# Value projection of two head pairs: from eight half products to seven, over the sums that queries and keys use

## The chip, the cores and the metric

The kernel runs on one NeuronCore of a Trainium2 chip. The metric is the device time of one execution in microseconds (us). Engines are named as the profile names them: PE is TensorE (matmul), PEld its weight loads, DVE is VectorE, ACT is ScalarE, POOL is GpSimd, SP is SyncE, which here only issues DMA transfers.

## What is computed

Two layers, each over four images of 1024 positions and 768 channels, all in float32:

```python
x = x + attention(_gn(x), ...)     # layer 0, then layer 1 with its own weights
# attention: q, k, v = split(xn @ Wqkv), 12 heads of 64
# scores = scale * q @ k.T + rel_h[..., :, None] + rel_w[..., None, :]
# out = softmax(scores) @ v ;  return out @ Wproj + bproj
```

`_gn` is a group normalisation over 32 groups of channels. The change concerns `v`, the values, alone.

## The kernel before, in words

**Units.** Heads go in pairs: `g` counts 48 pairs (8 images by 6 pairs, `NP`), and `pair` is the number within the image. A pair is worked in eight units `n` of 128 query rows. While unit (g, n) runs, the kernel also makes queries, keys and values of the next pair g + 1 and a part of the output projection. All engines run in the order in which the code emits their instructions (`tc.manual_schedule`); the Tile framework adds the semaphore waits.

**A unit, in the order of emission** (L740 to L826): DVE "between" instructions for groups that stand half done; the transfers collected in `early`; POOL's bias sums for two units ahead (`biases`, L429); the score matmuls of the next unit (L443) and their softmax (`exponentials`: DVE L455, ACT L459); then the first "piece" of projection work; `turn` (two DVE transposes L479 and the transfer of the result to DRAM, L481); `divide` for the next unit (DVE reciprocal L467, then products on ACT L473, one of the two on POOL L471 where n is 2 or 4 for the unit divided); POOL's weight differences (`combine` at n 0 and 1, `combine_values` at n 4 of odd pairs); the other pieces; and at n 2 and 6 `weigh`, the product of probabilities and values (L508, result `av`). At n 2 the position terms of the next pair (`positions`: 16 matmuls `tp`, L381, and the ACT copies `t` L386 and `raw` L389) stand ahead of the scores, at n 7 behind them.

**Pieces.** `plan` (L733) says which groups run in which unit: G0 to G3 are the four products of queries and keys (tile `pj`), V0 and V1 the values (tile `pv`), O0 and O1 the output projection (`oo`). A group made by `crossed` has two parts. In its first part, rows 0 to 63 of the array feed one half of the result tile and rows 64 to 127 the other; in the second part they change over. Ahead of the second part, `between` (L274) has DVE rewrite one element of a weight with itself, which makes PE wait until the first part has been read.

**Values before.** For every two head pairs, `project_values` makes four groups (i = 0 to 3), two of them beside an even pair and two beside an odd one. A group covers 256 positions by 256 output columns; each of its two parts has 12 matmuls of 64 rows x 256 moving columns, weights being the input `xn`. Two ACT copies (L366) bring the result into `v_of[g]` and `v_of[g + 1]`.

**Queries and keys** use a seven-product scheme: POOL makes differences of weights (`combine`, L129) and of inputs (`sums`, L257: s2, s3, s4 and an in-place x1 + x1), and DVE adds the products (L329). The sums of the next image are made at pairs 4 and 5 (`sum_steps`); s4 comes last, its three tiles at n 1 and n 2 of pair 5; before, its first reader is G3 at n 4.

**Places in PSUM.** The score tiles have two places (`ps_s`). Everything else (`pj`, `pv`, `oo`, `tp`, `av`) shares two places of pool `ps_m`. In the built program, a new tile takes the place that has been free longest. At n 2, group V1 stands half done and holds one of the two, so `tp` and then `av` take the other in turn.

**Transfers.** Each unit writes its transposed probabilities to DRAM (`td<-tb`, 1 MB) and reads them back one to three units later in another order (`pt<-td`, 1 MB, L490), all from SP in order; `weigh` at n 6 needs the reads of units 0 to 3.

## Time and profile before

| what | value |
|---|---|
| median of 3 runs | 3369.71 us (3365.89 to 3370.19) |
| profiled execution, own time | 3373.25 us |
| its span, first to last instruction | 3370.8 us |
| around the span | 2.45 us |
| PE / DVE / ACT / POOL busy | 98% / 72% / 61% / 69% |
| values: PE `pv`, 4608 records | 523.5 us |
| values: ACT copies L366, 192 | 59.8 us |
| values: POOL L140, 24 | 43.9 us |
| one pair of heads | 68.72 us in nearly all pairs |

The profile's first part gives the busy time of each engine; groups give line, engine, tiles, count, busy time and mean time of one; the timeline lists merged runs of instructions in order, with the start in us from the span's start, the duration, and in brackets the idle time of the engine before them and what ended it. One float32 matmul appears as two PE records. Matmuls on the upper and the lower 64 rows of the array run at once, so two records start almost together.

### The profile page before, as it was taken

To read this page: it belongs to the slowest core of one execution; us is meant where nothing else is said; L and a number is where in the kernel's file an instruction comes from. 1 tells how busy PE (TensorE), PEld (TensorE's weight loads), DVE (VectorE), ACT (ScalarE), POOL (GpSimd) and SP (SyncE) were. 2 spreads that over 40 slices of the span, in tenths; PEclk is the share of its full clock that TensorE was granted. 3 is DMA by queue.
4 is the path that set the end of the run, shared out by engine and by line. 5 is a ranking of instruction groups with operands and counts; after the bars stand their busy time and mean duration, and the time that the engine had idled before them with its cause. 6 is when DMAs were issued, how large, how long until landed. Compare 5 with 4: busy or idle time off the path is not lost.

```text
span 3370.8 us, 58086 instructions
## 1 busy us (share of the span) xinstructions
PE 3319.2 (98%) x21600; PEld 1875.8 (56%) x21600; DVE 2415.5 (72%) x3923; ACT 2039.6 (61%) x3140; POOL 2332.4 (69%) x1184
## 2 busy tenths in 40 slices
PE   6999999999999999999999999999999999999998
PEld 3555555555555555555555555555555555555554
DVE  3787677777777677777777777667776677767775
ACT  2666756566565666566655666566665657665563
POOL 5777866678666686666866668676686667766662
PEclk9999999999999999999999999999999999999999
DMA  3899989899998998889888999989998999898887
GB/s 113 297 330 312 336 306 338 319 306 335 321 322 314 315 331 312 312 300 334 320 309 315 316 321 330 317 306 313 337 313 308 334 306 335 301 324 299 312 290 263
DMA packets 534777, 1046.97 MB, mean 311 GB/s; under 512 B 149728, under 2 KB 212704, under 8 KB 485344
## 3 DMA queue, kind: packets, MB, share of 16 engines
q1 hardware_dynamic: 479936, 1015.84, 85.6%
q10 hardware_dynamic: 54560, 27.43, 2.8%
q8 instruction: 171, 2.80, 0.3%
q14 instruction: 110, 0.90, 0.1%
HBM read 568.01 MB, written 475.10 MB: 309 GB/s over the span
## 4 chain that ended last, share of the span: by engine, by line
PE 93%; DMA 4%; DVE 2%; issue 1%; ACT 0%; SPq 0%; POOL 0%; ACTq 0%; DVEq 0%
PE pj L285 21%; PE av L508 19%; PE s L443 19%; PE pv L285 15%; PE oo L285 13%; PE pj L313 3%; PE tp L381 3%; DMA td<-tb 2%; DMA pt<-td 1%; PE o L587 1%; DVE tb L479 1%; DMA xn<-in_x 0%; DVE sc L455 0%; DVE st L188 0%; DMA per<-mv 0%
## 5 line engine op out<-in xcount | busy, mean ns | idle before, releaser
L429 POOL TENSOR_TENSOR sc<-rel 128x1024 f32<-128x1024 f32 x768 | 1880.3, 2478 | 636.8 <-DVE tb L479 601.6
L455 DVE CUSTOM_DVE_ANT_0 sc<-s,sc 128x1024 f32<-128x1024 f32 x768 | 910.9, 1225 | 524.0 <-PE s L443 459.5
L459 ACT ACTIVATE sc<-sc,sm 128x1024 f32<-128x1024 f32 x768 | 878.5, 1146 | 484.9 <-DVE sm L455 483.8
L473 ACT ACTIVATE sc<-sc,sm 128x1024 f32<-128x1024 f32 x674 | 743.0, 1143 | 580.3 <-DVE sm L467 454.1
L479 DVE STREAM_TRANSPOSE tb<-sc 128x1024 f32<-128x1024 f32 x768 | 909.6, 1226 | 60.9 <-DMA td<-tb 56.8
L443 PE MATMUL s<-k,q 64*128 64x512 f32 x3072 | 738.6, 596 | 2.6 <-DVE sm L455 2.6
L508 PE MATMUL av<-pt,v 128*64 128x256 f32 x6144 | 687.5, 381 | 10.1 <-DMA pt<-td 9.0
L508 PEld LDWEIGHTS av<-pt,v 128*64 128x64 f32 x6144 | 436.2, 137 | 290.6 <-issue 48.5
L285 PE MATMUL pv<-wv,xn 64*128 64x256 f32 x4608 | 523.5, 376 | 1.0 <-DVE wv L274 1.0
L285 PEld LDWEIGHTS pv<-wv,xn 64*128 64x128 f32 x4608 | 447.7, 187 | 114.5 <-issue 55.2
L285 PE MATMUL oo<-attn,wo 64*128 64x512 f32 x2112 | 475.3, 589 | 0.0
L443 PEld LDWEIGHTS s<-k,q 64*128 64x128 f32 x3072 | 289.2, 187 | 316.1 <-issue 292.5
L285 PEld LDWEIGHTS oo<-attn,wo 64*128 64x128 f32 x2112 | 200.9, 187 | 228.0 <-issue 227.1
L471 POOL TENSOR_SCALAR sc<-sc,sm 128x1024 f32<-128x1024 f32 x94 | 105.1, 1118 | 305.7 <-DVE sm L467 295.6
L285 PE MATMUL pj<-xn,wa 64*128 64x512 f32 x1152 | 269.4, 598 | 30.6 <-DVE xn L235 26.7
L285 PE MATMUL pj<-xn,w 64*128 64x512 f32 x1152 | 263.3, 589 | 1.6 <-DVE w L274 1.6
L285 PE MATMUL pj<-s,wc 64*128 64x512 f32 x576 | 262.6, 589 | 0.0
L285 PE MATMUL pj<-s,w 64*128 64x512 f32 x576 | 262.6, 589 | 0.0
L285 PEld LDWEIGHTS pj<-xn,wa 64*128 64x128 f32 x1152 | 113.6, 189 | 166.5 <-issue 126.7
L285 PEld LDWEIGHTS pj<-xn,w 64*128 64x128 f32 x1152 | 111.6, 187 | 137.4 <-issue 134.9
L404 ACT COPY rel<-raw 32x256 f32<-32x256 f32 x384 | 155.1, 404 | 30.6 <-DMA part<-res 10.9
L285 PEld LDWEIGHTS pj<-s,wc 64*128 64x128 f32 x576 | 107.6, 187 | 67.6 <-issue 66.9
(68 smaller groups left out, 2118.5 us busy)
## 6 DMA issues: line engine op xcount, KB each, us to landing
td<-tb SPq DMA_DIRECT2D x384, 1024.0 KB, 6.6
pt<-td SPq DMA_DIRECT2D x382, 1024.0 KB, 9.0
tdr<-t ACTq DMA_DIRECT2D x96, 256.0 KB, 6.5
part<-res SPq DMA_DIRECT2D x84, 256.0 KB, 5.0
res<-part SPq DMA_DIRECT2D x84, 256.0 KB, 4.7
wa<-in_wqk SPq DMA_DIRECT2D x48, 384.0 KB, 3.3
wc<-in_wqk SPq DMA_DIRECT2D x48, 384.0 KB, 6.3
wv<-in_wv SPq DMA_DIRECT2D x24, 768.0 KB, 12.4
```

Source lines behind the costliest of these rows:

```text
L285: nc.tensor.matmul(to, lhsT=w, rhs=x, start=(half, at) == (0, 0), stop=(half, at) == (1, n - 1))
L313: nc.tensor.matmul(t[:, h, :], lhsT=w[rows, c, :], rhs=x[c][rows, :], start=(c == 0), stop=(c == NB - 1),)
L381: nc.tensor.matmul(ps[:, h, j, :], lhsT=q[rows, at * P : (at + 1) * P], rhs=tabs[l][rows, :], start=True, stop=True,)
L404: nc.scalar.copy(rel[rows, :, 0, :, :], raw[rows, :, :, WIDE - 1 - HW - y : WIDE - 1 - y])
L429: nc.gpsimd.tensor_tensor(sc.rearrange("p (a k) (u l) -> p a (k u) l", a=4, l=8), rel[:, h, 0, m, :].unsqueeze(1).unsqueeze(3).to_broadcas ...
L443: nc.tensor.matmul(ps[h][:, cols], lhsT=q[rows, n * P : (n + 1) * P], rhs=k[rows, cols], start=True, stop=True,)
L455: nc.vector.tensor_tensor_reduce(out=sc, in0=ps[h], in1=sc, scale=-scale, scalar=BIG, op0=ALU.add, op1=ALU.min, accum_out=st[:, 0, h : h + 1],
L459: nc.scalar.activation(sc, sc, AF.Exp, bias=st[:, 0, h : h + 1], scale=-1.0, accum_out=st[:, 1, h : h + 1],)
L471: nc.gpsimd.tensor_scalar(sc, sc, st[:, 2, h : h + 1], 1.0, ALU.mult, ALU.mult)
L473: nc.scalar.mul(sc, sc, st[:, 2, h : h + 1])
L479: nc.vector.transpose(tb[:, :, h, :], sc_of[g, n, h])
L508: nc.tensor.matmul(av[rows, at * 2 * P : (at + 1) * 2 * P], lhsT=v_of[g][:, k, rows], rhs=pt_of[g, quarter].rearrange("p n r k h i -> p (n ...
```

## The change

The values of two pairs (512 positions a half, 128 columns a pair, 384 channels a half) are made by the same seven-product scheme as queries and keys, with the same sums s2, s3, s4 and x1. `values` has kinds 0 to 3. Kinds 0, 1 and 2 are crossed groups with two products each, kind 3 is a single product without crossing. A product covers 512 positions by 128 columns over 384 channels, in matmuls of 64 rows x 128 moving columns; a crossed part has 24 of them, kind 3 has 24 in all. Beside an odd pair run kinds 0 (V0) and 3 (V1), beside an even pair kinds 1 (V0) and 2 (V1) of the two pairs begun before. The results are put together in the v tiles: kind 0 by one ACT copy and one DVE add, kind 3 by two DVE adds, kinds 1 and 2 by three DVE adds each (128 x 512).

The weight differences, one POOL subtraction of 128 x 768 before, become four of 128 x 384, two at n 3 and two at n 5 of an odd pair, with a new tile `wv2`. The order of pieces now depends on the pair: beside an odd pair, V1 no longer begins at n 1 and runs whole at n 3, behind G1. To make room, the small tile `g` of the normalisation moves into the place of `raw`. `between` touches an element of the moving operand for values (`kept` = 2), as it did. At the start of the program the order of the groups changes likewise.

```diff
-        wv_of[g] = w
+        wv_of[g] = w, wpool.tile([P, NB, P], FP, tag="wv2", name=f"wv2_{g}")
...
-    def combine_values(g):
-
-        w = wv_of[g]
-        nc.gpsimd.tensor_tensor(w[:, NB:], w[:, NB:], w[:, :NB], ALU.subtract)
+    def combine_values(g, stage):
+
+        w, t2 = wv_of[g]
+        sub = lambda to, x, y: nc.gpsimd.tensor_tensor(to, x, y, ALU.subtract)
+        w11, w21 = w[:, :NB, :P], w[:, NB:, :P]
+        w12, w22 = w[:, :NB, P:], w[:, NB:, P:]
+        if stage == 0:
+            sub(w11, w12, w11)
+            sub(w12, w22, w12)
+        else:
+            sub(t2, w22, w11)
+            sub(w21, w21, t2)
...
-        g = small.tile([NG, 2, GS, 2], FP, tag="g", bufs=1, name=f"g_{im}")
+        held = []
...
+            window = tmppool.tile([P, 2, 4, WIDE], FP, tag="raw", name=f"g_{im}")
+            g = window.rearrange("p h j r -> p (h j r)")[:NG, : 4 * GS]
...
-    def project_values(g, i):
+    def values(g, kind):
...
-        t = ps_m.tile([P, 2, HALF], FP, tag="m", name=f"pv_{g}_{i}")
-        yield from crossed(t, range(NC), lambda t, c, k, rows: (
-            t[:, k, : 2 * P], xn[c][rows, (2 * (i % 2) + k) * P : (2 * (i % 2) + k + 1) * P],
-            w[rows, c, :],
-        ), w[:, NC - 1, :])
-        for h in range(2):
-            nc.scalar.copy(v_of[g + h][:, 2 * i : 2 * i + 2, :], t[:, :, h * P : (h + 1) * P])
-        if i == 3 and g + 2 < NPAIR:
-            later.append(lambda: load_wv(g + 2))
...
+        t = ps_m.tile([P, 2, 4, P], FP, tag="m", name=f"pv_{g}_{kind}")
+        if kind == 3:
+            for b in blocks:
+                for c in range(NB):
+                    for h, rows in enumerate(ROWS):
+                        nc.tensor.matmul(
+                            t[:, h, b, :], lhsT=s4[c][rows, b * P : (b + 1) * P], rhs=w22[rows, c, :],
+                            start=(b, c) == (0, 0), stop=(b, c) == (3, NB - 1),
+                        )
+        else:
+            ops = {
+                0: ((w11, x0), (w21, x0[NB:])),
+                1: ((w2, s2), (w12, s3)),
+                2: ((w11, x1), (w21, x1[NB:])),
+            }[kind]
+            yield from crossed(t, [(b, c) for b in blocks for c in range(NB)], lambda t, bc, h, rows: (
+                t[:, h, bc[0], :], ops[h][1][bc[1]][rows, bc[0] * P : (bc[0] + 1) * P],
+                ops[h][0][rows, bc[1], :],
+            ), 2)
...
+        if kind == 0:
+            nc.scalar.copy(y10, ts[0])
+            add(y00, ts[1], y10)
+        elif kind == 3:
+            add(y01, ts[0], y10)
+            add(y01, ts[1], y01)
+        elif kind == 1:
+            add(y11, ts[0], y10)
+            add(y01, ts[0], y01)
+            add(y11, ts[1], y11)
+        else:
+            add(y10, ts[1], y11)
+            add(y01, ts[0], y01)
+            add(y11, ts[0], y11)
+            if g + 2 < NPAIR:
+                later.append(lambda: load_wv(g + 2))
...
-        first, i = (g - 1, 2) if g % 2 else (g, 0)
+        first, kinds = (g - 1, (1, 2)) if g % 2 else (g, (0, 3))
...
-        both("V1", "G1")
+        both("G1", "G2")
         later.pop(0)()
-        combine_values(0)
+        for stage in range(2):
+            combine_values(0, stage)
         load_w(1, "a")
-        now["G2"].part()
         now["G3"].part()
-        now["G2"].between()
-        now["G2"].part()
+        now["V1"].part()
...
-        plan = {
-            0: ("O1 previous", "G0", "V0"), 1: ("V0", "V1"), 3: ("V1", "G1"),
-            4: ("G1", "G3", "G2"), 5: ("G2", "O0"), 7: ("O0", "O1", "G0 next"),
+        same = {
+            0: ("O1 previous", "G0", "V0"), 4: ("G1", "G3", "G2"), 5: ("G2", "O0"),
+            7: ("O0", "O1", "G0 next"),
         }
+        plans = {**same, 1: ("V0", "V1"), 3: ("V1", "G1")}, {**same, 1: ("V0",), 3: ("G1", "V1")}
...
-            if n == 4 and pair % 2 and g + 1 < NPAIR:
-                combine_values(g + 1)
+            if n in (3, 5) and pair % 2 and g + 1 < NPAIR:
+                combine_values(g + 1, n // 4)
```

More of the change, by code (lines that the diff above doesn't have):

```diff
@@ L210, in by_group @@
         def by_group():
+            window = tmppool.tile([P, 2, 4, WIDE], FP, tag="raw", name=f"g_{im}")
+            g = window.rearrange("p h j r -> p (h j r)")[:NG, : 4 * GS]
+            g = g.rearrange("p (a k s) -> p a k s", a=2, s=2)
+            held.append(g)
             queue.dma_start(out=g[:, 0, :, :], in_=per.rearrange("(g k) s -> g k s", k=GS))
         def groups():
+            g = held[0]
             for k in range(2):
@@ L220, in inverses @@
         def inverses():
+            g = held[0]
             nc.vector.reciprocal(mv[:, 2, 0:1], mv[:, 2, 1:2])
@@ L274, in between, with crossed @@
             nc.vector.tensor_reduce(x, x, mybir.AxisListType.X, ALU.max)
-    def crossed(t, pairs, two, kept=None):
+    def crossed(t, pairs, two, kept=1):
         n = len(pairs)
@@ L280, in crossed @@
             for at in range(n):
+                at = n - 1 - at if half else at
                 for h in range(2):
                     h = h ^ half
-                    rows = ROWS[h ^ half]
-                    to, w, x = two(t, pairs[n - 1 - at if half else at], h, rows)
+                    to, w, x = two(t, pairs[at], h, ROWS[h ^ half])
                     nc.tensor.matmul(
-                        to, lhsT=w, rhs=x, start=(half, at) == (0, 0), stop=(half, at) == (1, n - 1)
+                        to, lhsT=w, rhs=x, start=at == half == 0, stop=at == 0 and half == 1
                     )
             if half == 0:
-                yield kept if kept is not None else two(t, pairs[n - 1], 1, slice(0, P))[1]
+                yield two(t, pairs[n - 1], 1, slice(0, P))[kept]
     def products(g, kind):
@@ L351, in products @@
                 later.append(lambda: load_w(g + 1, "c"))
-    def project_values(g, i):
-        im, pair = divmod(g, NP)
-        xn, w = xn_of[im][i // 2], wv_of[g]
-        if i == 0:
+    def values(g, kind):
+        im = g // NP
+        w, w2 = wv_of[g]
+        x0, x1 = xn_of[im]
+        s2, s3, s4 = ([sum_tiles.get((im, k, c)) for c in range(NB)] for k in (2, 3, 4))
+        if kind == 0:
             for h in range(2):
                 v_of[g + h] = vpool.tile([P, NT, P], FP, tag="v", name=f"v_{g + h}")
-        t = ps_m.tile([P, 2, HALF], FP, tag="m", name=f"pv_{g}_{i}")
-        yield from crossed(t, range(NC), lambda t, c, k, rows: (
-            t[:, k, : 2 * P], xn[c][rows, (2 * (i % 2) + k) * P : (2 * (i % 2) + k + 1) * P],
-            w[rows, c, :],
-        ), w[:, NC - 1, :])
-        for h in range(2):
-            nc.scalar.copy(v_of[g + h][:, 2 * i : 2 * i + 2, :], t[:, :, h * P : (h + 1) * P])
-        if i == 3 and g + 2 < NPAIR:
-            later.append(lambda: load_wv(g + 2))
+        w11, w21 = w[:, :NB, :P], w[:, NB:, :P]
+        w12, w22 = w[:, :NB, P:], w[:, NB:, P:]
+        blocks = range(4)
+        t = ps_m.tile([P, 2, 4, P], FP, tag="m", name=f"pv_{g}_{kind}")
[17 more added lines that the diff above has]
+            ), 2)
+        y00, y10 = v_of[g][:, :4], v_of[g][:, 4:]
+        y01, y11 = v_of[g + 1][:, :4], v_of[g + 1][:, 4:]
+        ts = [t[:, h] for h in range(2)]
+        add = lambda to, x, y: nc.vector.tensor_tensor(to, x, y, ALU.add)
+        if kind == 0:
+            nc.scalar.copy(y10, ts[0])
[13 more added lines that the diff above has]
+                later.append(lambda: load_wv(g + 2))
@@ L633, in prepare @@
     def prepare(g):
-        first, i = (g - 1, 2) if g % 2 else (g, 0)
+        first, kinds = (g - 1, (1, 2)) if g % 2 else (g, (0, 3))
         groups = {f"G{kind}": Crossed(lambda kind=kind: products(g, kind)) for kind in range(4)}
-        for k in range(2):
-            groups[f"V{k}"] = Crossed(lambda k=k: project_values(first, i + k))
+        for k, kind in enumerate(kinds):
+            groups[f"V{k}"] = Crossed(lambda kind=kind: values(first, kind))
         return groups
@@ L792, in attention_blocks @@
                 stages[n]()
-            pieces = [now[name] for name in plan.get(n, ()) if now.get(name)]
+            pieces = [now[name] for name in plans[pair % 2].get(n, ()) if now.get(name)]
             if n == 0 and len(pieces) == 2:
```

## The prediction

> **What bounds the kernel now.** I read the page's busy times and its chain first.

> ```profile
> PE 3319.2 (98%) x21600; PEld 1875.8 (56%) x21600; DVE 2415.5 (72%) x3923; ACT 2039.6 (61%) x3140; POOL 2332.4 (69%) x1184
> PE 93%; DMA 4%; DVE 2%; issue 1%; ACT 0%; SPq 0%; POOL 0%; ACTq 0%; DVEq 0%
> ```

> PE never rests, and the chain runs along it, so PE time saved is time saved, as long as nothing that PE waits for comes late. How near the others stand is read from the timeline of one even pair (unit 1 begins at 1015.89), engine by engine: first PE, then DVE, then ACT.

> ```profile
> 1015.89 1.88 PE L443 MATMUL s<-k,q 64*128 64x512 f32 x8
> 1017.61 5.35 PE L285 MATMUL pv<-wv,xn 64*128 64x256 f32 x48
> 1022.79 1.06 PE L381 MATMUL tp<-tab,q 64*128 64x128 f32 x16
> 1023.68 1.89 PE L443 MATMUL s<-k,q 64*128 64x512 f32 x8
> 1025.50 7.13 PE L508 MATMUL av<-pt,v 128*64 128x256 f32 x64
> ```

> ```profile
> 1020.21 2.37 DVE L479 STREAM_TRANSPOSE tb<-sc 128x1024 f32<-128x1024 f32 x2
> 1022.50 0.13 DVE L467 RECIPROCAL sm<-sm 128x2 f32<-128x2 f32 x1
> 1054.44 1.37 DVE L329 TENSOR_TENSOR k<-pj,k 128x512 f32<-128x512 f32 x2
> ```

> ```profile
> 1021.60 0.62 ACT L366 COPY v<-pv 128x256 f32<-128x256 f32 x2
> 1022.66 1.15 ACT L473 ACTIVATE sc<-sc,sm 128x1024 f32<-128x1024 f32 x1 [0.44 <-DVE sm L467]
> 1023.89 0.58 ACT L386 COPY t<-tp 128x512 f32<-128x512 f32 x1
> 1024.38 0.41 ACT L389 COPY raw<-tp 128x288 f32<-128x288 f32 x1
> ```

> `av` must wait for `raw` (group V1 stands half done in the other place): `raw` ends at 1024.79, `av` starts at 1025.50. The margin is 0.71 us, and nothing in the busy shares tells of it. Two more rows matter: POOL's s4 in a pair 5 (unit 1 there begins at 1223.53), and one place where PE already waits for a transfer.

> ```profile
> 1230.36 1.12 POOL L471 TENSOR_SCALAR sc<-sc,sm 128x1024 f32<-128x1024 f32 x1 [2.55 <-DVE sm L467]
> 1239.62 2.50 POOL L257 TENSOR_TENSOR s<-xn,s 128x512 f32<-128x512 f32 x2
> 1131.11 3.67 PE L508 MATMUL av<-pt,v 128*64 128x256 f32 x32 [1.05 <-DMA pt<-td]
> ```

> [...] the 16 `tp` records, 8 pairs of two, take 1023.68 − 1022.79 = 0.89 us[...]. [...] in `tp` the loads (187 ns each in the trace) stay hidden. [...] The trace shows every engine in emission order. [...]

> **PE's own work.** Before, a value part is 12 record pairs of 256 columns: half of the `pv` row, (1022.79 − 1017.61) / 2 = 2.59 us. After, it is 24 pairs of 128: 24 x 0.1115 = 2.68 us by `tp`. Two head pairs take 8 parts before, 20.72 us, and 7 after (kind 3 counts as one), 18.76 us: −1.96 us, times 24 = **−47.0 us**. It falls unevenly: beside an odd pair 2.59 − 3 x 0.09 = 2.3 us less, beside an even one 0.36 more.

> **Evictions.** Removed: 192 ACT copies (59.8 us busy). Added: 24 ACT copies of 0.58, and per two pairs nine DVE adds of 128 x 512 at about 0.69 (rows L329), 149 us of DVE busy in all. POOL gains 24 x (4 x 1.00 − 1.83) = 52 us. The shares have room. What counts is where they stand.

> *Even pair, unit 1.* All times from the unit's start. V0's second part runs from 1.72 to 4.40; a result is readable 0.22 after the next group's start (as at 1043.83 and 1044.05), so at 4.62. The softmax leaves DVE at 4.32. Three adds, 0.61 each (1.21 from 1054.44 to the next instruction, for two), end at 6.45. Only then come the transposes, which now start at 4.32; 2.29 later the reciprocal, 8.74; ACT's product at 8.90; `t` 1.05 later at 9.95 (two products take 2.09), `raw` from 10.44 to 10.85; weights and start 0.1. `av` could start at 4.40 + 2.68 + 0.89 + 1.82 = 9.79. PE waits 1.16 us, times 24 = **+27.8**. Behind it on PE stands everything, including the next scores.

> *Even pair, unit 3* (from 1032.56). V1's second part ends at 1.82 + 2.68 = 4.50; three adds from 4.72 to 6.55, transposes and reciprocal to 8.89, G1's between to 9.01, with 0.1 for the start 9.1. G1's second part could start at 4.50 + 2.57 + 1.72 = 8.79. PE waits 0.31, times 24 = **+7.4**. In six even pairs (pairs 0 and 2 of images 0 to 2) a statistics pair of 0.87 stands ahead of the between: **+5.2**.

> *Odd pair, unit 1.* V0 is kind 0: readable at 4.62, but ACT is in the softmax until 5.71 (1021.60); copy to 6.3, add to 7.03. `tp` takes the other place, `av` takes V0's, and could start at 4.40 + 0.89 + 1.82 = 7.11: about 0.1 lost. At n 3 V1's two adds end at 8.62 and the between at 8.8, against 8.79: 0.1. Together 23 x 0.2 = **+4.6**, and three odd pairs with statistics **+2.6**.

> *Pair 5.* V1 (kind 3) needs s4 at n 3, where before only G3 at n 4 did. The transposes of unit 1 start at 6.95 instead of 4.32, so POOL's product starts at 9.46 instead of 6.83 (1230.36), and the second s4 row ends 2.63 later than 1242.12: 21.22 from unit 1's start. PE comes to the third channel block at 5.29 + 8.87 + 1.82 + 2.57 + 0.45 = 19.0. It waits about 2.3, seven times: **+16.1**. If POOL had its sums earlier this would be nothing; it is no gain.

> **Transfers.** In unit 1 SP issues `td` at 10.44 (1026.33), behind eight position transfers, later than the delayed transposes end (8.74 or 9.24), so the queue keeps its time. From there to the landing of unit 3's read the DMA engines are full (page: mean 89%). PE comes 2.3 us sooner in odd pairs, the transfers don't. Between landing and the second half of `av` at n 6, seven of the odd pairs (1, 3, 9, 15, 19, 21, 27) have under 1 us; less 0.2 lost earlier, that is **+12.4**. Bounds: 0 if the queue moves with PE, and 2.1 in all 23, +48. In even pairs PE itself comes later: nothing. The normalisation's tile in `raw`'s place makes one transfer of seven images wait for ACT's position copies; the transfer ahead of it lands later still (28.6 against 24.6 from pair 15's start): nothing, at worst 1 us each.

> **Costs taken as nothing.** POOL's four differences at n 3 and 5 stand beside two bias sums of 4.9 in units of 7: hidden by POOL's waits for transposes (601.6 us in the waits), 1 us each without them. The start-up loses a value part, counted above.

> **Sum.** −47.0 + 27.8 + 7.4 + 5.2 + 4.6 + 2.6 + 16.1 + 12.4 = +29.1. The span goes from 3370.8 to 3400 and the profiled execution's own time from 3373.25 to 3402; on the median of the runs, 3369.7, that makes **3399 us**.

> **Rivals.**
> *A: PE stays the only bound* (faster). All evictions are covered, as the shares (DVE 72%, ACT 61%) suggest: 3369.7 − 47.0 = 3323. It decides if the three adds add less than the margin of 0.71 to the chain to `raw`; my walk gives them 2.13. A few waits on top make 3323 to 3362.
> *B: even.* The adds stall PE, but s4 and the transfers come in time (−28.5): 3371.
> *C: DMA becomes the bound.* With `pt` late in every odd pair, +36 on my sum: 3435. For it: DMA engines full for 25 us at a stretch; against it: 0.05 busy in the gaps.
> *D: the 128-column stream doesn't hold.* If each load's 187 ns set the pace, 24 x 168 x (0.187 − 0.1115) = 304 us more: about 3700. `tp` speaks against it, but only over 8 pairs in a row. Below 0.111 no reason leads.

> **How the numbers follow.** My case has a chance of 0.58 (3385 to 3418), A 0.18, B 0.09, C 0.12, D 0.03. Faster by over 0.2% is A; within 0.2% (6.7 us, about what a measurement of this kernel can tell from no change) is B; slower is the rest, 0.73. The range that holds 8 in 10 reaches from the upper end of A to most of C: 3352 to 3430.

> **What would show it.** Right: `pv` busy down to about 470 us; idle PE before `av` released by ACT `raw`, about 28 us in 24 waits; PE at G1's second part waiting for DVE, about 15; `pv` waiting for POOL L257, 16 in seven; `av` waiting for `pt`, 9 before, about 20; odd pairs near 66.6, even ones near 70.6. Wrong: if `raw` ends ahead of `av`'s natural start (the adds are shorter, or the place is another), A; if odd pairs wait for `pt` throughout, C; if `pv` starts come at more than 0.112, D.

## The result, and the profile after

The changed kernel takes 3383.34 us in the median of six runs (3381.66 to 3389.19), the kernel before 3369.78 us beside it: a ratio of 1.0045 with a 95% interval of 1.0033 to 1.0057, 13.6 us slower. The forecast was 3399 us, slower. The profiled span went from 3370.8 to 3380.3 us: 9.5 us between two single executions, against 13.6 between the medians.

The page of the changed kernel, busy times and chain:

```profile
PE 3287.5 (97%) x25056; PEld 1878.3 (56%) x25056; DVE 2550.3 (75%) x4115; ACT 1992.7 (59%) x2972; POOL 2383.3 (71%) x1256
PE 78%; DMA 8%; DVE 7%; POOL 3%; issue 2%; ACT 2%; SPq 1%; ACTq 0%; DVEq 0%; POOLq 0%
```

PE is busy for 31.7 us less than before, although the span is 9.5 us longer: idle time of PE grew by 41 us. The chain, 93% PE before, now passes over DVE, POOL, ACT and the transfers. The timeline shows where. Unit 1 of the even pair that the prediction walked through begins at 1014.34 now; first PE, then DVE, then ACT:

```profile
1016.05 2.84 PE L299 MATMUL pv<-wv,s 64*128 64x128 f32 x48
1018.73 2.85 PE L299 MATMUL pv<-wv,xn 64*128 64x128 f32 x48
1021.41 1.06 PE L430 MATMUL tp<-tab,q 64*128 64x128 f32 x16
1022.30 1.89 PE L492 MATMUL s<-k,q 64*128 64x512 f32 x8
1025.16 1.08 PE L557 MATMUL av<-pt,v 128*64 128x256 f32 x8 [0.97 <-ACT raw L438]
```

```profile
1018.95 1.89 DVE L401 TENSOR_TENSOR v<-pv,v 128x512 f32<-128x512 f32 x3 [0.21 <-PE pv L299]
1020.75 2.36 DVE L528 STREAM_TRANSPOSE tb<-sc 128x1024 f32<-128x1024 f32 x2
1023.03 0.12 DVE L516 RECIPROCAL sm<-sm 128x2 f32<-128x2 f32 x1
```

```profile
1023.19 1.15 ACT L522 ACTIVATE sc<-sc,sm 128x1024 f32<-128x1024 f32 x1 [3.12 <-DVE sm L516]
1024.24 0.57 ACT L435 COPY t<-tp 128x512 f32<-128x512 f32 x1
1024.71 0.40 ACT L438 COPY raw<-tp 128x288 f32<-128x288 f32 x1
```

A value part takes 1018.73 − 1016.05 = 2.68 us. From the unit's start, the adds run from 4.61, the transposes from 6.41, the reciprocal comes at 8.69, `raw` ends at 10.77 and `av` starts at 10.82; without the wait, PE's own work would have let it start at 9.79. Before, the same marks were: no adds, 4.32, 6.61, 8.90 and 9.61.

In unit 4 of the same pair, G1's second part waits for the between. DVE comes to that only after three adds (from 1036.93), the transposes and, in this pair, the statistics; DVE, then PE:

```profile
1041.06 0.67 DVE L196 BATCH_NORM_STATS2 st<-xn 128x6 f32<-128x512 f32 x1
1041.89 0.11 DVE L288 TENSOR_REDUCE wc<-wc 128x1 f32<-128x1 f32 x1
```

```profile
1042.06 0.69 PE L299 MATMUL pj<-s,wc 64*128 64x512 f32 x1 [0.88 <-DVE wc L288]
```

Such a unit 4 is 0.93 or 1.15 us longer than before, in six even pairs; in the other 18, without statistics, it is 0.34 longer.

The waits of PE in the changed kernel (time in total, times, longest):

```profile
PE av L557 <- ACT raw L438: 22.4, 23, 1.0
PE pv L384 <- POOL s L271: 12.0, 14, 1.0
PE pj L299 <- DVE wc L288: 7.7, 10, 1.3
PE av L557 <- DMA pt<-td: 4.9, 5, 1.5
```

The second line is V1 of the pairs 5. In the pair whose unit 1 begins at 1223.53, POOL's queue and the matmuls that wait for it:

```profile
1232.90 1.14 POOL L520 TENSOR_SCALAR sc<-sc,sm 128x1024 f32<-128x1024 f32 x1 [5.16 <-DVE sm L516]
1242.12 2.52 POOL L271 TENSOR_TENSOR s<-xn,s 128x512 f32<-128x512 f32 x2
```

```profile
1243.45 0.49 PE L384 MATMUL pv<-wv,s 64*128 64x128 f32 x4 [0.98 <-POOL s L271]
1244.69 4.13 PE L384 MATMUL pv<-wv,s 64*128 64x128 f32 x40 [0.74 <-POOL s L271]
```

POOL's product starts 9.37 us after the unit's start (6.83 before), and the last s4 tile is ready at 21.1 (18.6 before), while PE stands waiting for it.

Where the time went, in us, from the start of the first score matmul of every unit in both traces. The last row is what the others leave over:

| term | forecast | measured in the profiles |
|---|---|---|
| PE's work, start-up included | −47.0 | −50.0: even pairs 24 x +0.36, odd 23 x −2.32, start-up −5.2 |
| even pairs, n 2 (`av` for `raw`) | +27.8 | +24.0 |
| even pairs, n 4 (G1 for its between) | +12.6 | +12.3 |
| odd pairs, n 2 and n 4 | +7.2 | +6.5 |
| pairs 5, n 3 (V1 for s4) | +16.1 | +17.3 |
| transfers, seen at n 6 and n 7 | +12.4 | +2.4 |
| first pairs, last pair and tail | 0 | −3.0 |
| sum | +29.1 | +9.5 |

### The profile page after: what moved, and what is told of

Read it like the earlier page. It is cut to its first block, busy times and chain, and to the rows that moved or that the text cites. A ratio compares the mean times of both kernels' runs of the same rounds, so it can differ in the third digit from the quotient of the medians.

```text
span 3380.3 us, 64943 instructions
## 1 busy us (share of the span) xinstructions
PE 3287.5 (97%) x25056; PEld 1878.3 (56%) x25056; DVE 2550.3 (75%) x4115; ACT 1992.7 (59%) x2972; POOL 2383.3 (71%) x1256
## 4 chain that ended last, share of the span: by engine, by line
PE 78%; DMA 8%; DVE 7%; POOL 3%; issue 2%; ACT 2%; SPq 1%; ACTq 0%; DVEq 0%; POOLq 0%
PE pj L299 18%; PE av L557 15%; PE s L492 15%; PE oo L299 13%; PE pv L299 9%; DMA td<-tb 6%; DVE tb L528 4%; PE pj L327 3%; PE tp L430 2%; POOL sc L478 2%; PE pv L384 2%; DVE v L401 1%; DMA pt<-td 1%; PE o L636 1%; POOL s L271 1%
## 5 line engine op out<-in xcount | busy, mean ns | idle before, releaser
L508 ACT ACTIVATE sc<-sc,sm 128x1024 f32<-128x1024 f32 x768 | 878.5, 1146 | 348.5 <-DVE sm L504 346.7
L528 DVE STREAM_TRANSPOSE tb<-sc 128x1024 f32<-128x1024 f32 x768 | 908.8, 1225 | 60.2 <-DMA td<-tb 55.6
L299 PEld LDWEIGHTS pv<-wv,xn 64*128 64x128 f32 x4608 | 272.3, 188 | 35.6 <-issue 25.9
L299 PE MATMUL pv<-wv,xn 64*128 64x128 f32 x4608 | 274.7, 272 | 1.0 <-DVE wv L288 1.0
L401 DVE TENSOR_TENSOR v<-pv,v 128x512 f32<-128x512 f32 x216 | 140.2, 686 | 72.6 <-ACT v L403 43.6
## 6 DMA issues: line engine op xcount, KB each, us to landing
wv<-in_wv SPq DMA_DIRECT2D x24, 768.0 KB, 12.4
```

The costliest lines, as they stand in the source:

```text
L299: nc.tensor.matmul(to, lhsT=w, rhs=x, start=at == half == 0, stop=at == 0 and half == 1)
L401: add = lambda to, x, y: nc.vector.tensor_tensor(to, x, y, ALU.add)
L508: nc.scalar.activation(sc, sc, AF.Exp, bias=st[:, 0, h : h + 1], scale=-1.0, accum_out=st[:, 1, h : h + 1],)
L528: nc.vector.transpose(tb[:, :, h, :], sc_of[g, n, h])
```

## The experiments

All ratios are to the kernel before, run beside it; the changed kernel stands at 1.0045. A hundredth of the ratio is 34 us. Each kernel has one profiled execution; the sums by unit are from that one.

**The order on ACT.** The copies `t` and `raw` go ahead of ACT's softmax product of unit 2; DVE keeps its order.

```diff
+    delayed = []
...
+            elif n == 2:
+                delayed.append(lambda sc=sc, r=st[:, 2, h : h + 1]: nc.scalar.mul(sc, sc, r))
...
             if n == 2:
                 early_positions.clear()
+                run(delayed)
```

> One edit on the changed kernel: ACT's softmax product for unit 2 is emitted behind the position copies t and raw at n 2, not ahead of them. The three adds stay ahead of the transposes. Theory (the adds delay the reciprocal, the reciprocal delays ACT's product, and the copies stand behind that product): raw ends at about 9.1 us from unit 1's start instead of 10.78, av starts at its natural 9.79, the 1.04 us wait of PE goes in all even pairs, 23 x 1.04 = 24 us: about 3359, faster than before. Rival 1 (the adds are simply too much DVE work, the order on ACT doesn't matter): no change, 3383. Rival 2 (the transfers take over as soon as PE runs ahead): at most half of it, 3371, with more waits of av for pt.

Measured: 0.9984 (0.9976 to 0.9991), 21 us less than the changed kernel and faster than before. ACT, and then PE, in the same even pair (unit 1 begins at 1015.08):

```profile
1023.26 0.59 ACT L435 COPY t<-tp 128x512 f32<-128x512 f32 x1 [2.46 <-PE tp L430]
1023.75 0.40 ACT L438 COPY raw<-tp 128x288 f32<-128x288 f32 x1
```

```profile
1024.87 1.51 PE L561 MATMUL av<-pt,v 128*64 128x256 f32 x11
```

`raw` ends 9.07 us after the unit's start and `av` starts at 9.79, its natural place. In every even pair but the first, which has no `av` at n 2, n 2 is 1.04 shorter, 24.0 us together. The theory holds, and rival 1 falls. Rival 2 allowed at most half of the gain; the timed runs gave 21 of 24 us. The profiled execution, though, was the slowest of the twenty (3378.75 against a median of 3367.00), and in it the odd pairs gave 22.8 us back. That is more than the waits explain, and n 6 of pair 15 shows why. Its `av` row, which waited for `pt`, and then two windows (start:end, length, PE busy and its instructions, the same of PEld, DVE, ACT and POOL, granted clock, DMA share, GB/s):

```profile
1132.12 5.36 PE L561 MATMUL av<-pt,v 128*64 128x256 f32 x32 [2.63 <-DMA pt<-td]
```

```profile
1124.00:1130.00 6.00, 5.50 (x42) 2.79 (x38) 4.76 (x8) 3.48 (x5) 4.61 (x2) 1.00 1.04 358
1133.50:1137.00 3.50, 3.50 (x21) 2.50 (x20) 2.42 (x3) 0.00 (x0) 1.10 (x1) 0.56 0.39 157
```

The 32 matmuls take 5.36 us instead of 3.67: by the clock record of this trace, PE runs at half clock for 3.41 us from 1133.2, within this row. Seven such stretches lie in odd pairs between 3 and 31, with 1.7 us lost in each. Over the span the half clock cost 17.6 us here and 1.7 in the changed kernel's profile. The median of the timed runs, 21 us better, shows that not every run loses so much.

**The sums on POOL.**

```diff
-        (4, 7): ((1, 1), (2, 1)),
-        (5, 0): ((3, 2), (1, 2), (2, 2)),
-        (5, 1): ((4, 0),),
-        (5, 2): ((4, 1), (4, 2)),
+        (4, 7): ((1, 1), (2, 1), (4, 0)),
+        (5, 0): ((3, 2), (1, 2), (2, 2), (4, 1)),
+        (5, 1): ((4, 2),),
```

> One edit on the changed kernel: the three s4 tiles of the next image are made one step earlier each (pair 4 n 7, pair 5 n 0, pair 5 n 1). Theory (V1 of pair 5 waits for POOL's s4): unit 3 of the pairs 5 goes from 9.59 back to 7.08 us, seven times 2.25 less (one of them 3.9) = 16 to 18 us: about 3366. Rival (those units are late for another reason, such as the slower rate of the kind 3 matmuls or the POOL queue as a whole): no change, 3383, or the same time lost at another place where POOL's bias sums come 1.3 us later.

Measured: 1.0002 (0.9994 to 1.0011), 14.5 us less than the changed kernel. In the trace n 3 of the pairs 5 is shorter by 17.4 us in all, and no `pv` matmul waits for POOL. The pairs 5 lose 0.67 us each at n 4 instead, 4.7 together: at n 3 half of DVE's softmax waits 1.17 us for POOL's bias sums, and G1's between comes after it. The theory holds, and a quarter of the gain is lost. That is not the last clause of the rival, for the sums come no later by this edit: they start 13.77 us after the start of unit 1 in both kernels (11.18 in the kernel before), and DVE waited for them in the changed kernel too, where PE's wait for s4 covered it.

**The adds behind the transposes.**

```diff
-            if n == 0 and len(pieces) == 2:
+            if n == 0 and len(pieces) == 2 or pair % 2 == 0 and n in (1, 3):
                 pieces.insert(0, None)
```

> One edit on the changed kernel: in even pairs the value pieces at n 1 and n 3 are emitted behind the transposes and the reciprocal, so DVE transposes first and adds afterwards; PE's order stays. Theory (the adds have no good place: ahead they hold up the copies, behind they hold up V0's place in PSUM): at n 1 the reciprocal is back at 6.6 us, but V0's place comes free at 8.6 and the position matmuls, natural at 7.08, wait about 1.5 us instead of av's 1.04 (+12 us in all); at n 3 G1's second part no longer waits 0.34 (-8 us). Net +2 to +6 us: 3385 to 3389. Rival (only the order adds before transposes costs): -24 - 8 = 3351.

Measured: 1.0091 (1.0072 to 1.0110), 15.5 us more than the changed kernel; 2 to 6 were expected. DVE and PE of the same pair (unit 1 begins at 1017.96):

```profile
1024.57 0.12 DVE L516 RECIPROCAL sm<-sm 128x2 f32<-128x2 f32 x1
1024.61 1.86 DVE L401 TENSOR_TENSOR v<-pv,v 128x512 f32<-128x512 f32 x3
```

```profile
1026.62 1.16 PE L430 MATMUL tp<-tab,q 64*128 64x128 f32 x16 [1.42 <-DVE v L401]
```

The reciprocal is back at 6.61, and now `tp` waits for V0's place: 1.66 us longer at n 1, 1.01 shorter at n 2, 0.29 shorter at n 4. Even pairs come out 9.8 us longer, which is more than expected, and odd ones 10.9, mostly at n 6 and n 4 (`av` waits for `pt` 12.3 us in this trace, 4.9 in the changed kernel's). The rival, that only the order of adds before transposes costs, falls: behind them the adds cost more.

**Two of three adds left out.**

```diff
-            add(y11, ts[0], y10)
-            add(y01, ts[0], y01)
-            add(y11, ts[1], y11)
+            add(y11, ts[1], y10)
...
             add(y10, ts[1], y11)
-            add(y01, ts[0], y01)
-            add(y11, ts[0], y11)
```

> Two of the three DVE adds of kinds 1 and 2 are left out, so the values are incomplete and the output is not the reference's; all matmuls stay. It takes away the suspected cost. Theory: the chain to raw and the one to G1's between shorten by 1.22 us each, more than the waits of 1.04 and 0.34, so both vanish: -24 - 8 = about 3351, the remaining distance to the full PE saving (3323) being the s4 waits and the startup. Rival (DVE's load or the transfers bound the pair): less than a third of it, above 3373.

Measured: 0.9938 (0.9917 to 0.9959), 36 us less than the changed kernel. In the trace, n 2 of even pairs is 24.0 us shorter and n 4 12.3, to the hundredth what the changed kernel had lost there. PE's waits for `raw` are gone. The theory holds, and the rival, a gain under a third of this, falls.

**The adds doubled.** The first add of kinds 1 and 2 is done four times, to the same sum.

```diff
-            add(y11, ts[0], y10)
+            for _ in range(4):
+                add(y11, ts[0], y10)
...
-            add(y10, ts[1], y11)
+            for _ in range(4):
+                add(y10, ts[1], y11)
```

> One edit on the changed kernel: the first add of kinds 1 and 2 is done four times (the same sum each time), so six adds stand where three stood. Theory: the waits of PE in even pairs grow by the added 1.83 us each, from 1.04 to 2.87 at n 2 and from 0.34 to 2.17 at n 4, 24 x 3.66 = 88 us, and since the transfers then have more time, the waits of odd pairs for td's place and for pt go (5 to 10 us): 3460 to 3472. Rival (some of the adds is hidden, or the transfers bind the odd pairs whatever the even ones do): under 3440, or odd pairs unchanged.

Measured: 1.0390 (1.0373 to 1.0407), 116 us more than the changed kernel; 88 less a little was expected. The profile says where the rest is. Each repeated add writes over the result of the one before and takes 0.725 us to the next, not 0.61, so three of them add 2.18. At n 1 and n 2 together even pairs are 2.18 us longer. The expectation had the wait at `av` alone; by now it is 1.82 at `tp`, which waits for V0's place, and 0.36 at `av`. At n 4 twelve of the 24 pairs are 2.18 longer and twelve 3.9 or more. One of these, PE's row after the wait, and the windows before and after it:

```profile
1518.41 0.69 PE L299 MATMUL pj<-s,wc 64*128 64x512 f32 x1 [2.24 <-DVE wc L288]
```

```profile
1514.30:1521.20 6.90, 4.66 (x20) 1.87 (x18) 6.34 (x11) 2.82 (x4) 2.80 (x2) 0.87 0.38 148
1521.20:1523.20 2.00, 2.00 (x8) 0.77 (x6) 0.20 (x1) 0.71 (x2) 2.00 (x2) 0.60 0.47 111
```

Again half the clock for 3.41 us, 1.70 us lost. All in all 24 x 4.36 = 105 us of waits and about 12 x 1.7 = 20 of half clock, of 127 in the profile's even pairs. None of the adds is hidden. The other half of the expectation fell: the odd pairs' waits did not go when the even pairs had more time (`av` for `pt` 5.0 us, against 4.9; DVE's transposes for `td`'s place 52.8 against 55.6).

**The statistics.**

```diff
-                c = n - 2 if pair == 0 else loads.get((pair, n - 2), loads.get((pair - 1, n + 6), -1))
-                if pair < 3 and c >= 0:
-                    stats(im + 1, c, 1 if pair == 0 else 0, xn_of[im + 1][0][c])
...
             if n not in (2, 6):
                 held = []
+            if im + 1 < B:
+                c = n - 2 if pair == 0 else loads.get((pair, n - 2), loads.get((pair - 1, n + 6), -1))
+                if pair < 3 and c >= 0:
+                    stats(im + 1, c, 1 if pair == 0 else 0, xn_of[im + 1][0][c])
```

> One edit on the changed kernel: the statistics of the next image's input (0.68 + 0.2 us on DVE) are emitted behind the between of the held groups, not ahead of it. Theory (at n 4 G1's second part waits for DVE, and nine times the statistics stand in that chain): unit 4 of pairs 0, 1 and 2 in images 0 to 2 goes from 10.4 (even) and 10.4 (odd) back to 9.8 and 9.6, nine times 0.8 = 7 us: about 3376. Rival (the wait is for the matmuls of G1's first part): no change.

Measured: 1.0043 (1.0027 to 1.0059), no difference to the changed kernel that could be told. In the trace n 4 is shorter in all nine units with statistics, by 0.55 to 0.83 us, 6.6 together, as the theory says. But n 4 of other odd pairs is 3.1 us longer and n 6 of odd pairs 4.9, with 11.5 us of `av` waiting for `pt` in this execution. So the place is shown, and a gain in time is not: a wait went and others came.

**The three together.** The order on ACT, the sums and the statistics.

> The three edits together on the changed kernel: copies ahead of ACT's product, s4 a step earlier, statistics behind the between. If the waits were independent: -24 - 17 - 7 from 3383 = 3335. Theory after the first four runs (each us that PE gains in the even pairs is partly given back in the odd ones, where transposes wait for td's place and av for pt): a third to a half of it comes back, 3345 to 3357, still faster than before. Rival (the transfers bind all pairs): not under 3362.

Measured: 3346.66 us against 3374.39 before, 0.9921 (0.9907 to 0.9936): a version faster than both, and within the 3345 to 3357 that were expected. The waits of PE in it that bear on this:

```profile
PE pj L299 <- DVE wc L288: 11.4, 16, 2.2
PE av L561 <- DMA pt<-td: 5.8, 7, 1.2
```

Those for `raw` and for s4 are gone. What remains is G1's between, 0.34 in nearly all even pairs and up to 4.1 us in single odd ones. The largest is in pair 15: the transposes of unit 3 wait for `td`'s place, that landing comes 7.25 us after the unit's start, and the transposes start at 7.34 instead of 4.42. PE then waits 2.2 us and loses 1.7 to half clock.

**Behind it: n 3 alone with the piece behind the transposes.**

> The three edits, and in even pairs at n 3 alone the value piece behind the transposes, which takes G1's wait of 0.34 away (24 times 0.3 = 7 us) and lets td leave 2 us sooner. Theory: 5 to 10 us under the kernel with the three edits. Rival (the transfers bind): the same as that one within 0.2%.

Measured: 0.9930 (0.9915 to 0.9945), the same as the three edits. In the trace the 0.31 us went from n 4 in sixteen even pairs, as expected. In the seven pairs 4 beside which the next image is normalised, n 4 became up to 3.6 us longer, 6.0 together, so the even pairs come out even; the odd ones are 4.3 us longer. DVE in pair 10 (unit 3 begins at 747.03):

```profile
756.64 0.17 DVE L518 RECIPROCAL sm<-sm 128x2 f32<-128x2 f32 x1 [2.84 <-ACT sc L508]
756.73 1.86 DVE L401 TENSOR_TENSOR v<-pv,v 128x512 f32<-128x512 f32 x3
```

ACT has three normalisations (2.21 us) ahead of its softmax there, and DVE's reciprocal waits for that softmax, as it does in all seven (0.3 to 2.8 us). The adds now stand behind the reciprocal. So the rival's number came, and at these seven places its reason is not the whole one: DVE's order, with the reciprocal ahead, holds the adds up.

**Less traffic.** The last kernel without the writes of the partial sums; the layer's input is read in their place.

```diff
-            src = srcs[l][b] if p == 0 else part_of[im]
+            src = srcs[l][b]
...
-        if not end:
+        if not end and p:
             early.append(lambda: nc.sync.dma_start(out=dst, in_=to))
+        elif not end:
+            pass
```

> The kernel before this one in the list, with 84 of its transfers left out: the partial sums of the output projection are not written to DRAM, and the first half of each sum is read from the layer's input instead (so the output is not the reference's). That is 22 MB of 1047, 2% of the traffic, with PE, DVE, ACT and POOL unchanged. Theory (odd pairs are late by transfers): waits of av for pt and the late transposes of odd pairs shrink, 8 to 20 us less than the same kernel with them, 3325 to 3340. Rival (the waits left are of the engines' order): the same within 0.2%.

Measured: 0.9910 (0.9892 to 0.9929); medians 3341.5 and 3349.6, 8 us, at the edge of what was expected and with intervals that overlap. In the trace n 4 becomes 13.8 us shorter and n 6 3.8 longer. Of the 13.8, 8.5 are in the seven pairs 4 just named: in pair 10 ACT no longer waits for a transfer (4.51 us in the kernel above) ahead of its position copies. That transfers make up part of what remains is likely, and not shown by the times.

**The narrow matmul alone.** The kernel before, its value matmuls cut into two of 128 columns.

```diff
-        yield from crossed(t, range(NC), lambda t, c, k, rows: (
-            t[:, k, : 2 * P], xn[c][rows, (2 * (i % 2) + k) * P : (2 * (i % 2) + k + 1) * P],
-            w[rows, c, :],
-        ), w[:, NC - 1, :])
+        yield from crossed(t, [(c, j) for c in range(NC) for j in range(2)], lambda t, cj, k, rows: (
+            t[:, k, cj[1] * P : (cj[1] + 1) * P],
+            xn[cj[0]][rows, (2 * (i % 2) + k) * P : (2 * (i % 2) + k + 1) * P],
+            w[rows, cj[0], cj[1] * P : (cj[1] + 1) * P],
+        ), w[:, NC - 1, P:])
```

> The kernel before, with its value matmuls cut in two: 64 x 128 moving columns instead of 64 x 256, twice as many, all else as it was. It prices the narrow matmul alone. Theory: each of 192 parts takes 24 x 0.1115 = 2.68 instead of 2.59 us: +17 us, 3387 against 3370. Rival (weight loads set the pace over 24 pairs in a row): a pair at 0.187, +350 us; or no cost at all, 3370.

Measured: 1.0038 (1.0025 to 1.0052), 13 us with an interval of 8 to 18; in the trace even pairs are 10.1 and odd ones 8.3 us longer, 0.09 to 0.10 a part. Its group:

```profile
L285 PE MATMUL pv<-wv,xn 64*128 64x128 f32 x9216 | 540.1, 272 | 1.0 <-DVE wv L274 1.0
```

The weight loads stay hidden over 24 and 48 record pairs in a row: a part grows by the 0.09 to 0.10 us above, although a load's record takes 188 ns, longer than the 0.111 us from one pair to the next.

## Why the prediction was right, and where it was off

The direction, the places and most sizes were right. The size of the whole was not: +29.1 forecast, +13.6 measured, and 3383.34 lies 1.7 us below the range that the prediction gave its own case. In the profiles the sum is 19.6 us lower. About half of that is the transfers; the rest is the even pairs' `av` (3.8), PE's work (3.0), and the first and last pairs (3.0). The direction doesn't hang on the transfers: without them the forecast was +16.7.

**PE's own work** was right: 2.68 us a part, 2.32 us less beside odd pairs and 0.36 more beside even ones, priced apart by the cut matmuls. It rests on the `tp` row alone: 0.89 us for 8 pairs of records, 0.111 from one pair to the next, and 6 to 7 ns between the starts of the two in a pair. The start-up was counted as one value part and gained 5.2 us instead of about 2.3: two PE waits that the old order of groups had there (1.58 for G2's between, 1.18 at `tp`) are gone, and one of 0.60 is new.

**The eviction chain** was right in mechanism and place, and nearly in size. The walk gave adds to 6.45, reciprocal 8.74, `raw` 10.85, `av` 10.95; the trace has 6.41, 8.69, 10.77 and 10.82. Of the 0.13 us too much, 0.08 is in the rows up to `raw` and 0.05 in the 0.1 for "weights and start". It was also multiplied by 24, while the first pair has no `av` at n 2. Taking adds away and putting the copies first moved PE by what the walk says; adding more did so with the measured 0.725 us a step; putting the adds behind moved the wait to another instruction. So the loss is neither DVE's load (75% busy) nor the order on DVE alone. Three adds lengthened by 1.87 us a chain that had 0.71 us of margin, and by its own condition rival A fails.

**G1's between and the odd pairs** came within 1 us of their sums. For the even pairs that is the walk. For the odd ones it is partly luck: of +2.3 at n 2 nothing came (−0.6), and n 4 took 7.1 instead of 4.9.

**s4** was right: about 2.25 us in six pairs 5, and in one 3.9, of which 1.7 is half clock (from 1244.90 to 1248.10 the granted clock is 0.50). Made earlier, the wait goes.

**The transfers are the step that failed.** It said that between unit 1 and the landing of unit 3's read the DMA engines are full (89% busy in the profile before), that the landings stay while PE comes 2.3 us sooner in odd pairs, and that seven pairs with under 1 us of margin lose 12.4 us. The trace shows +2.4. From unit 1's start that read lands at 42.3 us on average over the odd pairs before and 41.8 after, and between 41.8 and 42.4 in the experiments: on average it does stay. But a single pair's landing moves by 2 us and more from one profile to another (pair 15: 46.4 before, 42.8 after, 46.7 with the copies first). In the changed kernel's profile the seven landed 1.0 to 3.6 us sooner, at 43.0 on average instead of 45.3, just as PE came at 43.0; two of them waited, 1.2 us together, and of the other pairs, some of which landed later, 7 and 25 waited 1.5 and 1.2. The seven are a late group in the other traces too: 43.5 to 44.7 on average, against 40.9 to 41.6 for the other odd pairs. So it was right that they are the late ones, and wrong to take 45.3 of one execution for their place. What moves single landings was not found; whether they move as much between two executions of one kernel isn't shown either, since each has one profile. More time in the even pairs, which I supposed midway, is not it: with the doubled adds the seven land at 44.1. The lateness also shows at a place that the step didn't name, n 4, through `td`'s place.

**Rivals.** B, with s4 and transfers free, would have been 3371; s4 was not free. C did not come. In the profiles of the experiments part of a gain is often given back in the odd pairs, but the timed runs don't show that as a rule: with the waits for `raw`, s4 and statistics removed, 42 of about 48 us (24 + 17 + 7) remain, and the 4.7 us that the pairs 5 lose at n 4 to POOL's late bias sums are most of the rest. D falls.

## What to carry to other kernels

An engine at 75% busy, as DVE was here, can still be the one that PE waits for: take the margin at the instruction that PE needs next (0.71 us here), and walk each engine's queue, in the order in which the trace shows it run, with the added instructions in it (here 1.87 us of adds), row by row. When evictions move from one engine to another, ask what stands behind them in the new queue and who waits for that; here putting two copies ahead of a product that PE did not need yet turned a loss of 0.45% into a gain of 0.16%. Don't take transfer margins from one profile where landings move by more than the margin from one to another.

## What the runs showed of the hardware that was not expected

The DVE adds of 128 x 512 of kinds 1 and 2, none of which reads or writes the result of the one just before it, follow each other at 0.60 to 0.61 us in the changed kernel's trace. Where each writes over the last one's result (the doubled adds), or reads it (kind 3), they follow at about 0.725.
